# Convolution and state projections of a scan block on tiles of the TensorE array, with other ranks

## The chip, the cores and the metric

The kernel runs on one core of a Trainium2 chip. The metric is device time in microseconds for one call, the median of three runs. A separate execution was recorded by the profiler; its own time and its span are given beside the runs, and all durations of single instructions come from it.

## The reference

The input `x` is 8 images of 96 channels and 64 x 64 positions (L = 4096), in f32. There are two layers. The first is a selective-scan block:

```python
xh = _layernorm(transpose(_gn(x)))
xi, z = split(xh @ in_proj_w.T + in_proj_b, 2)            # 192 channels each
xi = silu(depthwise_conv3x3(xi, conv_w) + conv_b)
xs = [xi by rows, xi by columns, and both reversed]       # k = 0..3
dts, Bs, Cs = split(einsum('bkdl,kcd->bkcl', xs, x_proj_w), [6, 22])
delta = softplus(einsum('bkrl,kdr->bkdl', dts, dt_proj_w) + dt_proj_b)
h = exp(delta * A) * h + delta * xs * Bs                  # 16 states, along L
y = sum(h * Cs) + Ds * xs                                 # the four k summed back in place
out = (layernorm(y) * silu(z)) @ out_proj_w.T + out_proj_b
x = x + out
```

The second layer takes tokens t of 96 channels: an attention without softmax (so keys and values reduce to one 96 x 96 matrix per image), then a feed-forward of 384 hidden units whose operands are rounded to an 8-bit float. Both are added to t.

## The kernel before

The images are worked in four pairs. The channels of a pair, 2 x 192, are held as three tiles of 128 partitions, T = 0, 1, 2: T = 0 has the first 128 channels of one image, T = 1 those of the other, T = 2 the last 64 of each. Positions go in chunks of F = 512 (eight rows of an image), so an image has NCH = 8 chunks.

**Stages.** For each pair there is a front part, then a scan, then a back part. The program alternates: a stage with the front part of pair 0; a scan; three middle stages in which the back part of one pair and the front part of the next are mixed; a scan after each; and a last stage with only a back part. The scan (`scan`) is a loop written out by hand and is not touched.

**The front part** consists of `project`, `convolve` and `prepare`. `project` normalises chunks and multiplies them with the input weights (three matmuls a chunk), writing `xi` into padded images `pad[T]` and the gate `z` to DRAM. `convolve` does the 3 x 3 depthwise convolution. T = 0 and T = 2 are done on VectorE, nine passes over half an image each (L521, L524). T = 1 is done on TensorE (L532): per chunk nine matmuls with diagonal 128 x 128 weights (`diag`, made at L506) into one PSUM bank, evicted by ScalarE with the bias; then one ScalarE SiLU per chunk and T. `prepare` works on 32 sets (k, c), direction k and chunk c. A set does three matmuls (L594) of 128 x 76 weights into one bank: B, C and the 6 rank rows of both images, summed over T. ScalarE copies the 76 rows to `S`. B and C go to DRAM (`bs`, `cs`). Three matmuls with 12 rows (L606) give the step sizes of each T. For each T follow a softplus, a product `du` on VectorE (L611), and a split of the f32 step into three bf16 parts: ScalarE copy, VectorE difference (L622), ScalarE copy, GpSimd difference (L627). They go to DRAM as `du` and `dl`. For the column directions (k = 1, 3), GpSimd first makes the transposed chunk (L586).

**The back part** consists of `back` and `tail`. `back` works on 16 units (chunk and image): it reads the scan's `ys`, adds directions (L923, on VectorE and GpSimd), transposes by matmuls with the identity (`turn`, L937, into `py` banks), normalises, gates and projects out (`both`, L956), normalises again and builds keys and values (`keys`, L989; `outer`, L996; copies to `kv`). When all 16 units are done, `hm` is formed, and `tail` does 16 units of attention and feed-forward (L1046, L1054, L1065), each with a norm (L394, L398).

**Order.** Within a stage no order is written by hand. Each operation is recorded in a `Plan` with its engine, an assumed cost, what it reads and writes, the rings of buffers it takes from, and a rank. `Plan.run` then simulates the engines: for each engine it takes, among the operations that could start within 0.1 us of the earliest, the one with the lowest rank, and emits it. So each engine's queue is an order that was fixed when the program was built, and each engine executes it strictly in turn. All DMAs are issued by SyncE's queue. The ranks of a stage run from 0 to about 1, and constants set where each part lies: the front up to FRONT, convolution to CONV, sets from PREP to 1, back up to BACK, tail from TAIL to TAIL_END. A change of SiLU, softplus or logarithm costs ScalarE a table load.

**PSUM** has eight banks. In a middle stage there are rings `q` (3), `hold` (2) and `py` (2), and `pm` has one. The convolution and L594 use `py` in a middle stage and `hold` in the first.

## Time and profile before

| what | us |
|---|---|
| median of 3 runs (10441.0 to 10453.86) | 10443.78 |
| the profiled execution | 10465.3 |
| its span | 10463.5 |
| first stage, to the first scan instruction | 571 |
| each scan | 1778 |
| each middle stage | 784, 788, 785, and 25 to the next scan |
| last stage | 346 |

Busy over the whole span: PE (matmul) 7723.3 us, VectorE 9031.7, ScalarE 6996.6, GpSimd 8006.9; the DMA queue's packets take 76.2% of the 16 engines' span.

A line of a group gives source line, engine, operation, the tiles written and read by the program's names, the shape, the count, then busy us and mean ns of one, then the idle time of the engine just ahead of it and what ended that. An f32 matmul stands in the profile as two records. Lines of helpers stand for many calls: L287 is every ScalarE activation, L306 every DMA of a stage. `A` is a slab that holds many tiles of the front part. In rows by stretches of time, the columns are from and to, the length, then busy time with the number of instructions for PE, PE weight loads, VectorE (DVE), ScalarE (ACT) and GpSimd (POOL), then the TensorE clock granted as a share of full speed, the mean busy share of the DMA engines, and GB/s.

### The profile page before, as it was taken

The numbers are of one execution on the slowest core, as the hardware profiler recorded it, in microseconds if no ns is written. First come the engines' busy times: TensorE is split into PE (matmuls) and PEld (weight loads), VectorE is DVE, ScalarE is ACT, GpSimd is POOL, SyncE is SP. The second block draws the span as 40 slices with busy tenths as digits, with TensorE's granted clock in tenths as the row PEclk, the third lists the DMA queues.
The fourth block names the chain that finished last, engine by engine and source line by source line (L and its number), as shares of the span: only waits on it lengthen the run. The fifth ranks groups of instructions, "written<-read, shape, count | busy, mean of one in ns | idle before, by whom it ended". The sixth has DMA issues, their size and how long they took to land. (4 is left out here: it accounts for less than half of the span.)

```text
span 10463.5 us, 377190 instructions
## 1 busy us (share of the span) xinstructions
PE 7723.3 (74%) x163328; PEld 5391.4 (52%) x163328; DVE 9031.7 (86%) x6692; ACT 6996.6 (67%) x12229; POOL 8006.9 (77%) x2799
## 2 busy tenths in 40 slices
PE   7856667668986667666997666666699766666678
PEld 2245556554425556555432555555543255555554
DVE  6589999997569999999655999999865699999985
ACT  4567777765666777776666777777656677777754
POOL 3489999990349999998133999999713499999971
PEclk8689898999878998998986889998898699989889
DMA  4888888877868888887686888888767688788884
GB/s 119 213 212 215 213 215 213 217 193 158 217 164 214 212 216 214 215 216 191 164 211 163 212 212 216 215 213 215 191 166 207 167 214 214 215 216 213 215 194 104
DMA packets 1590580, 2082.95 MB, mean 199 GB/s; under 512 B 406579, under 2 KB 1047092, under 8 KB 1585332
## 3 DMA queue, kind: packets, MB, share of 16 engines
q1 hardware_dynamic: 1588916, 2058.80, 76.2%
q8 instruction: 1283, 21.02, 0.9%
q14 instruction: 381, 3.12, 0.1%
HBM read 1600.53 MB, written 457.72 MB: 197 GB/s over the span
## 5 line engine op out<-in xcount | busy, mean ns | idle before, releaser
L794 DVE TENSOR_TENSOR_SCAN h<-da,dbu 128x774 f32<-128x774 f32 x4096 | 7027.0, 1759 | 132.2 <-POOL dbu L758 30.7
L758 POOL TENSOR_TENSOR dbu<-dut,bc 128x1536 f32<-128x1536 f32 x2048 | 7082.5, 3547 | 68.4 <-DMA cw<-cs 23.3
L783 ACT ACTIVATE da<-da 128x768 f32<-128x768 f32 x4092 | 3260.4, 797 | 1995.4 <-PE da L776 1985.5
L776 PE MATMUL da<-dm,aw 128*128 128x128 bf16 x24576 | 2288.5, 236 | 2270.9 <-DVE h L794 2056.7
L776 PEld LDWEIGHTS <-aw 128*128 128x128 bf16 x24576 | 1794.5, 104 | 2516.7 <-issue 2212.3
L812 PE MATMUL yp<-h,cw 128*32 128x48 f32 x131072 | 2910.7, 239 | 86.9 <-issue 73.3
L812 PEld LDWEIGHTS yp<-h,cw 128*32 128x32 f32 x131072 | 2417.0, 154 | 537.4 <-issue 220.7
L712 ACT ACTIVATE cw<-bc,blk 128x512 f32<-128x512 f32 x2048 | 1472.7, 720 | 76.1 <-DMA dm<-dl 57.0
L627 POOL TENSOR_TENSOR A<-A 128x512 bf16<-128x512 f32 x384 | 469.4, 1226 | 960.3 <-ACT A L287 940.3
L287 ACT ACTIVATE A<-A 128x512 bf16<-128x512 f32 (+2 forms) x809 | 486.2, 619 | 235.3 <-DVE A L622 229.9
L923 POOL TENSOR_TENSOR yd<-yk 128x768 f32<-128x768 f32 x64 | 131.1, 2048 | 626.8 <-DMA yk<-ys 357.1
L606 PE MATMUL q<-A 12*128 12x512 f32 x768 | 517.5, 786 | 57.2 <-ACT A L287 50.7
L820 ACT ACTIVATE yev<-yp 128x384 f32<-128x384 f32 x1024 | 504.7, 493 | 65.2 <-PE yp L812 64.8
L622 DVE TENSOR_TENSOR A<-A 128x512 f32<-128x512 f32 x384 | 338.6, 887 | 206.0 <-ACT A L287 193.5
L586 POOL COPY A<-A 128x512 f32<-128x512 f32 x96 | 143.0, 1501 | 364.8 <-ACT A L287 318.7
L755 ACT COPY dbu<-h 128x12 f32<-128x12 f32 x1984 | 409.5, 206 | 0.0
L606 PEld LDWEIGHTS q<-A 12*128 12x128 f32 x768 | 147.3, 223 | 368.0 <-ACT A L287 209.0
L937 PEld LDWEIGHTS py<-ident,yd 128*96 128x96 f32 x2048 | 262.8, 176 | 134.7 <-issue 89.7
L611 DVE TENSOR_TENSOR A<-A 128x512 f32<-128x512 f32 x192 | 188.4, 989 | 149.1 <-ACT A L287 148.6
L1073 POOL TENSOR_TENSOR yk<-yk,yd 96x512 f32<-96x512 f32 x64 | 89.7, 1404 | 294.4 <-DVE yd L1071 240.9
L937 PE MATMUL py<-ident,yd 128*96 128x128 f32 x2048 | 284.9, 291 | 24.7 <-DVE yd L923 11.2
L524 DVE SCALAR_TENSOR_TENSOR A<-A,c_convw,A 128x2048 f32<-128x2048 f32 x128 | 299.6, 2380 | 0.2
(131 smaller groups left out, 5916.1 us busy)
## 6 DMA issues: line engine op xcount, KB each, us to landing
dut<-du SPq DMA_DIRECT2D x2048, 384.0 KB
dm<-dl SPq DMA_DIRECT2D x1024, 288.0 KB
dl<-A SPq DMA_DIRECT2D x256, 384.0 KB
dm<-dl SPq DMA_DIRECT2D x1024, 96.0 KB
ys<-yev SPq DMA_DIRECT2D x1024, 96.0 KB
du<-A SPq DMA_DIRECT2D x256, 256.0 KB
bc<-cs SPq DMA_DIRECT2D x512, 128.0 KB
bc<-bs SPq DMA_DIRECT2D x512, 128.0 KB
```

What stands on the lines that cost most here:

```text
L287: "ACT", cost, lambda: nc.scalar.activation(dst(), src_(), func, **kw),
L606: mm(P, 1.0, lambda pq=pq, k=k, T=T, S=S: nc.tensor.matmul(P[pq], dtw[64:76, k, T], P[S][64:76], start=True, stop=True), (S, "dtw"), (pq,) ...
L627: P.add("POOL", 1.24, lambda rest=rest, dp=dp, w=w: nc.gpsimd.tensor_tensor(P[dp][:, :, 2], w(rest), P[dp][:, :, 1], ALU.subtract), (rest, ...
L712: nc.scalar.activation(cw[i % 2][:, :, :, m, :].rearrange("p z j t -> p (z j) t"), bc[i][:, 1].rearrange("p z (j t) -> p (z j) t", j=NB), ...
L755: nc.scalar.copy(start, segs(hs[s - 1][:, :, r])[:, :, :, 1 if back else TC])
L758: nc.gpsimd.tensor_tensor(segs(t)[:, :, :, 1:], dut[g].unsqueeze(1) .to_broadcast([128, 2, NI, TC]), bc[s // NB][:, 0, :, bass.ts(c % NB, ...
L776: nc.tensor.matmul(e[:, i], aw[k, r][:, i, z, :], dm[s // 2][:, NI * r + i, bass.ts(c % 2, TC)], start=True, stop=True,)
L783: nc.scalar.activation(e, e, AF.Exp)
L794: nc.vector.tensor_tensor_scan(hs[s][:, w, r][:, d], da[p % 3][:, o : o + W6][:, d], dbu[4 * s + r][:, w][:, d], 0.0, ALU.mult, ALU.add,)
L812: nc.tensor.matmul(y[32 * q : 32 * q + 32, 2 * NE * i : 2 * NE * i + 2 * NE] .rearrange("p (j r i) -> p i j r", j=2, r=NR), w[:, z, :, t], ...
L820: nc.scalar.activation(yev[s][:, :, o : o + 8, :].rearrange("p j i e -> p i j e"), y[:, 0 : 16 * NE].rearrange("p (i j e) -> p i j e", j=2 ...
L937: nc.tensor.matmul(o, P[yd][:, k, j, DIM * g : DIM * g + DIM], ident, start=(k + j == 0), stop=(k + j == 4),)
```

## The change

The convolution of T = 1 no longer uses 128 x 128 diagonal weights but 32 x 32 ones (`diag` is 128 x 9 x 32). Four chunks of an image half are done in one block (`taps`): for each of nine taps, 16 matmuls, one for each group i of 32 channels and each chunk j. Channel group i is rows 32i of the array and writes bank i; chunk j is columns 32j and partitions 32j of the bank. The block needs four banks at once. ScalarE evicts each 32-partition piece with SiLU and bias directly (bias from `cbr`, laid out for it), so the separate SiLU of T = 1 falls away.

In `prepare`, the first product (`states`) puts one image into columns 0 to 63 and the other into columns 64 to 127: two matmuls for T = 0 and T = 1 side by side, then two for T = 2. The bank has 128 rows, in which each image's 6 rank rows come first and then B and C; these go to DRAM in two DMAs each instead of one. The weights `xw` grow from 76 to 128 columns; they are prepared once in `weights`. The second product (`steps_`) is six matmuls of 6 rows and 64 columns at rows 0, 64, 32 and 96 of the array, into three banks. `dtw` is loaded in four pieces to these rows. A ring `set` lets two sets be between `states` and `steps_` at a time.

`Plan` gets `claims`: a claimed operation that is ready but short of banks keeps operations of higher rank from taking banks of that ring. The banks are now `q` (5) and `hold` (2), with 3 `hold` in the first stage; `py` is gone. The ranks FRONT, CONV, PREP, BACK, TAIL and TAIL_END have other values.

```diff
@@ -36,12 +36,12 @@
 SEG = TC + 1
 W6 = NI * SEG
 HQ = TC // 4
-FRONT = 0.22
-CONV = 0.28
-PREP = 0.24
-BACK = 0.65
-TAIL = 0.54
-TAIL_END = 0.65
+FRONT = 0.13
+CONV = 0.27
+PREP = 0.15
+BACK = 0.63
+TAIL = 0.85
+TAIL_END = 1.33
 NE = 24
 X0 = F - 3 * SEG
...
         self.unit = self.also = None
+        self.claims = set()
...
@@ -108,7 +109,12 @@
                 heirs[j].append(i)
         ready = [i for i, n in enumerate(owed) if not n]
         while ready:
-            best = {}
+            best, claimed = {}, {}
+            for i in self.claims & set(ready):
+                rings = [self.home[n] for n in self.ops[i][4] if n not in self.tiles]
+                for ring in set(rings):
+                    if len(self.free[ring]) < rings.count(ring):
+                        claimed[ring] = min(claimed.get(ring, 9.0), self.ops[i][5])
             for i in ready:
                 engine, cost, _, after, uses, rank, kind, _ = self.ops[i]
...
@@ -116,7 +122,7 @@
                 for ring in {self.home[n] for n in uses if n not in self.tiles}:
                     want = sum(self.home[n] == ring for n in uses if n not in self.tiles)
                     slots = sorted(f[0] for f in self.free[ring])
-                    short |= len(slots) < want
+                    short |= len(slots) < want or (i not in self.claims and rank > claimed.get(ring, 9.0))
                     at = max([at] + slots[:want])
                 if short:
...
     convw = load("convw", [128, 2, 9], -0.8)
     convb = load("convb", [128, 2], 0.1)
+    cbr = const.tile([128, 4], F32, name="cbr")
+    for j in range(4):
+        lay(cbr[32 * j : 32 * j + 32], a["convb"][:, 0:1].rearrange("(i p) o -> p (i o)", i=4), 0.1, "cb")
...
         for out_, in_, rank, name, after in later:
             dma(P, 0.1, lambda out_=out_: out_, lambda in_=in_: in_, after, (f"w_{name}",), (), rank)
-        xw = wp.tile([128, KD, 3, 76], F32, name="xwp")
+        xw = wp.tile([128, KD, 3, 128], F32, name="xwp")
+        P.add("POOL", 1.4, lambda: nc.gpsimd.memset(xw, 0.0), (), ("xwp",), (), -0.5)
+        parts = []
...
+        dma(P, 0.79, lambda: xwd, lambda: xw, parts, ("xwd",), (), 0.1)
...
-        diag = p1.tile([128, 9, 128], F32, name="diag")
-        for t in range(9):
-            dve(P, 0.28, lambda t=t: nc.vector.tensor_scalar(
-                diag[:, t, :], ident, convw[:, 0, t : t + 1], None, ALU.mult), ("w_convw",), (f"diag#{t}",), (), -0.5)
+        diag = p1.tile([128, 9, 32], F32, name="diag")
+        for g in range(4):
+            g4 = slice(32 * g, 32 * g + 32)
+            dve(P, 0.45, lambda g4=g4: nc.vector.tensor_tensor(
+                diag[g4], ident[g4, g4].unsqueeze(1).to_broadcast([32, 9, 32]),
+                convw[g4, 0].unsqueeze(2).to_broadcast([32, 9, 32]), ALU.mult),
+                ("w_convw",), (f"diag.{g}",), (), -0.5)
         for h in range(2):
             first = FRONT + (CONV - FRONT) * h / 2
...
                             o, v, w, o, ALU.mult, ALU.add), (), wr, (), first + (CONV - FRONT) / 2 * (9 * (T // 2) + t) / 18)
-            for c in range(4 * h, 4 * h + 4):
-                first = FRONT + (CONV - FRONT) * c / 8
-                r0 = c * ROWS
-                n = f"pc.{c}"
+            first = FRONT + (CONV - FRONT) * h / 2
+            ns = [f"pc{h}{i}" for i in range(4)]
+
+            def taps(h, ns):
                 for t in range(9):
                     dy, dx = divmod(t, 3)
-                    mm(P, 0.87, lambda n=n, t=t, r0=r0, dy=dy, dx=dx: nc.tensor.matmul(
-                        P[n], diag[:, t, :], pad[1][:, r0 + dy : r0 + dy + ROWS, dx : dx + HH],
-                        start=(t == 0), stop=(t == 8)), (f"diag#{t}", "edge1", *[f"pad1#{j}" for j in range(NCH)]), (n,), ((n, "py" if beside else "hold"),), first)
-                act(P, lambda c=c: xi[1][:, bass.ts(c, F)], lambda n=n: P[n], AF.Identity, 0.68, (n, "A1.1", "w_convb"),
-                    (f"xi1#{c}",), (), first, bias=convb[:, 0:1])
+                    for j in range(4):
+                        r0 = (4 * h + j) * ROWS + dy
+                        for i in range(4):
+                            g4 = slice(32 * i, 32 * i + 32)
+                            nc.tensor.matmul(
+                                P[ns[i]][32 * j : 32 * j + 32], diag[g4, t],
+                                pad[1][g4, r0 : r0 + ROWS, dx : dx + HH], start=(t == 0), stop=(t == 8),
+                            )
+
+            P.claims.add(len(P.ops))
+            mm(P, 9.0, lambda h=h, ns=ns, taps=taps: taps(h, ns),
+               ("edge1", *[f"pad1#{c}" for c in range(NCH) if h or c <= NCH // 2],
+                *[f"diag.{g}" for g in range(4)]), ns, [(n, "q") for n in ns], first)
+            for i in range(4):
+                for j in range(4):
+                    g4 = slice(32 * i, 32 * i + 32)
+                    j4 = slice(32 * j, 32 * j + 32)
+                    act(P, lambda g4=g4, c=4 * h + j: xi[1][g4, bass.ts(c, F)], lambda n=ns[i], j4=j4: P[n][j4],
+                        AF.Silu, 0.6, (ns[i], "A1.1", "w_cb"), (f"xi1#{4 * h + j}.{i}",), (), first,
+                        "silu", bias=cbr[j4, i : i + 1])
         P.also = None
         for c in range(NCH):
-            for T in range(3):
-                b_ = 0.0 if T == 1 else convb[:, half(T) : half(T) + 1]
+            for T in (0, 2):
+                b_ = convb[:, half(T) : half(T) + 1]
                 act(P, lambda T=T, c=c: xi[T][:, bass.ts(c, F)], lambda T=T, c=c: xi[T][:, bass.ts(c, F)],
                     AF.Silu, 0.72, ("w_convb",), (f"xi{T}#{c}",), (), FRONT + (CONV - FRONT) * (0.5 if c < 4 else 1), "silu", bias=b_)
+
...
         P.also = "A2" if beside else "A3"
-        xw = tmp.tile([128, KD, 3, 76], F32, name="xw")
-        dma(P, 0.5, lambda: xw, lambda: xwd, ("xwd",), ("xw",), (), -1)
-        dtw = tmp.tile([128, KD, 3, 128], F32, name="dtw")
-        dma(P, 0.1, lambda: dtw[64:76], lambda: a["dtw"].rearrange("k r t c -> r k t c"), (), ("dtw",),
-            (), -1)
+        xw = tmp.tile([128, KD, 3, 128], F32, name="xw")
+        dma(P, 0.79, lambda: xw, lambda: xwd, ("xwd",), ("xw",), (), -1)
+        dtw = tmp.tile([128, KD, 128], F32, name="dtw")
+        places = ((0, 0, 0, 0, 128), (64, RK, 1, 0, 128), (32, 0, 2, 0, 64), (96, RK, 2, 64, 64))
+        for at, r, T, o, n in places:
+            dma(P, 0.03, lambda at=at, o=o, n=n: dtw[at : at + RK, :, o : o + n],
+                lambda r=r, T=T, o=o, n=n: a["dtw"][:, r : r + RK, T, o : o + n].rearrange("k r c -> r k c"),
+                (), (f"dtw{at}",), (), -1)
         ring(P, tmp, "S", 2, [128, F])
+        P.ring("set", [None] * 2)
         for T in range(3):
...
                     pt, S = "pt" + n, "S" + n
-                    for T in range(3):
-                        mm(P, 1.0, lambda pt=pt, k=k, T=T, f=u[T]: nc.tensor.matmul(
-                            P[pt][:76], xw[:, k, T], f(), start=(T == 0), stop=(T == 2)),
-                           (un[T], "xw"), (pt,), ((pt, "py" if beside else "hold"),), rank)
-                    act(P, lambda S=S: P[S][:76], lambda pt=pt: P[pt][:76], AF.Copy, 0.59, (pt,), (S,),
+
+                    def states(pt, k, u):
+                        for last in (False, True):
+                            for b in range(2):
+                                h = slice(64 * b, 64 * b + 64)
+                                nc.tensor.matmul(
+                                    P[pt][h], xw[:, k, 2 if last else b, h], u[2 if last else b](),
+                                    start=not last, stop=last,
+                                )
+
+                    P.unit = f"set.{k}.{c}"
+                    mm(P, 1.9, lambda pt=pt, k=k, u=u, states=states: states(pt, k, u),
+                       (*un[0], *un[1], *un[2], "xw"), (pt,), ((pt, "q"),), rank)
+                    act(P, lambda S=S: P[S], lambda pt=pt: P[pt], AF.Copy, 0.59, (pt,), (S,),
                         ((S, "S"),), rank)
-                    for v, r in ((bs, 0), (cs_, 32)):
-                        dma(P, 0.07, lambda v=v, k=k, c=c: v[k, 2 * c : 2 * c + 2].rearrange("j p t -> p j t"),
-                            lambda S=S, r=r: P[S][r : r + 32].rearrange("p (j t) -> p j t", j=2),
-                            (S,), (), (), rank)
+                    for v, r in ((bs, RK), (cs_, 32 + RK)):
+                        for b in range(2):
+                            dma(P, 0.035, lambda v=v, k=k, c=c, b=b: v[
+                                    k, 2 * c : 2 * c + 2, NS * b : NS * b + NS].rearrange("j p t -> p j t"),
+                                lambda S=S, r=r, b=b: P[S][64 * b + r : 64 * b + r + NS].rearrange(
+                                    "p (j t) -> p j t", j=2), (S,), (), (), rank)
+                    pqs = [f"pq{n}.{T}" for T in range(3)]
+
+                    def steps_(pqs, k, S):
+                        for at, T, o in ((0, 0, 0), (0, 0, 64), (64, 1, 0), (64, 1, 64), (32, 2, 0), (96, 2, 64)):
+                            nc.tensor.matmul(
+                                P[pqs[T]][o : o + 64], dtw[at : at + RK, k, o : o + 64], P[S][at : at + RK],
+                                start=True, stop=True,
+                            )
+
+                    mm(P, 1.2, lambda pqs=pqs, k=k, S=S, steps_=steps_: steps_(pqs, k, S),
+                       (S, *[f"dtw{at}" for at, *_ in places]), pqs, [(q, "q") for q in pqs], rank)
+                    P.unit = None
                     for T in range(3):
                         m = f"{n}.{T}"
                         pq, d, q, dp, rest = "pq" + m, "d" + m, "du" + m, "dp" + m, "rest" + m
-                        mm(P, 1.0, lambda pq=pq, k=k, T=T, S=S: nc.tensor.matmul(
-                            P[pq], dtw[64:76, k, T], P[S][64:76], start=True, stop=True),
-                           (S, "dtw"), (pq,), ((pq, "q"),), rank)
                         act(P, lambda d=d: P[d], lambda pq=pq: P[pq], AF.Softplus, 0.675, (pq, "w_dtb"), (d,),
                             ((d, "d"),), rank, "softplus", bias=dtb[:, k, half(T) : half(T) + 1])
...
                 for g in range(2):
                     py = f"py{g}" + n
                     mm(P, 1.0, lambda yd=yd, k=k, g=g, py=py, turn=turn: turn(yd, k, g, py), (f"{yd}#{k}",),
-                       (py,), ((py, "py"),), rank)
+                       (py,), ((py, "q"),), rank)
             for g in range(2):
...
             P = Plan()
             tmp = st.enter_context(tc.tile_pool(name="bk", bufs=1))
             if new and old:
-                psum = banks(P, st, q=3, hold=2, py=2)
+                psum = banks(P, st, q=5, hold=2)
             elif new:
-                psum = banks(P, st, q=4, hold=4)
+                psum = banks(P, st, q=5, hold=3)
             else:
-                psum = banks(P, st, q=3, hold=2, py=2)
+                psum = banks(P, st, q=5, hold=2)
```

## Prediction

> **What bounds the kernel now.** I read the page first, then the busy time by stage, then one middle stage cut at its own events, then its groups of instructions and its waits.
>
> The page, parts 1 and 2:
>
> ```profile
> PE 7723.3 (74%) x163328; PEld 5391.4 (52%) x163328; DVE 9031.7 (86%) x6692; ACT 6996.6 (67%) x12229; POOL 8006.9 (77%) x2799
> ...
> PE   7856667668986667666997666666699766666678
> ...
> DVE  6589999997569999999655999999865699999985
> ...
> PEclk8689898999878998998986889998898699989889
> ```
>
> The shares of the whole mislead: DVE's 86% are the four scans. In the dips of the DVE row (slices 10-12, 20-22, 30-32) PE shows 7 to 9. By stage: 0 to 571 us the first front stage, four scans of 1778 us, three middle stages (2349 to 3133, 4936 to 5724, 7530 to 8315, each with 25 us to the next scan), the last stage 346 us. The scans are built from the same instructions after the change, so I take nothing from them, and the last stage's order on PE is the same with other PSUM tiles; both count as 0. What can move is 3 x 785 us and 571 us.
>
> One middle stage, cut at the first matmul, the first and last convolution matmul, the end of the back part, and the scan; columns are time, length, then busy us (instructions) of PE, weight loads, DVE, ACT, POOL, then clock, DMA share, GB/s:
>
> ```profile
> 2372.00:2551.00 179.00, 167.27 (x627) 87.69 (x628) 131.22 (x162) 123.80 (x191) 19.31 (x10) 0.96 0.84 186
> 2551.00:2629.00 78.00, 77.97 (x223) 36.94 (x222) 46.31 (x30) 33.08 (x48) 5.82 (x6) 1.00 0.37 91
> 2629.00:2937.00 308.00, 286.34 (x779) 119.78 (x780) 171.25 (x221) 196.45 (x319) 103.21 (x80) 0.84 0.82 215
> 2937.00:3133.00 196.00, 168.57 (x294) 50.64 (x293) 121.87 (x210) 134.91 (x223) 71.98 (x56) 0.71 0.58 156
> ```
>
> PE is 86 to 100% busy in all four phases, 705 of 784 us, and no other engine is above 74% in any. PE sets this stage. But DMA is second: 0.82 at 215 GB/s in the third phase, and 0.71 over the stage, which is 557 us of work at full share. That is the next floor. The groups that the change touches, in the same stage:
>
> ```profile
> L606 PE MATMUL q<-A 12*128 12x512 f32 x192 | 125.8, 767 | 9.5 <-ACT A L287 7.4 <-DVE yk L1048 1.6 <-ACT small L287 0.3
> ...
> L532 PE MATMUL py<-A,diag 128*128 128x512 f32 x144 | 63.4, 592 | 0.0
> L594 PE MATMUL py<-A 128*76 128x512 f32 x96 | 60.8, 741 | 0.9 <-POOL A L586 0.9
> ...
> L594 PE MATMUL py<-A,A 128*76 128x512 f32 x96 | 55.7, 703 | 2.6 <-DVE yt L949 1.9 <-ACT A L287 0.7
> ```
>
> Each f32 matmul is two records, so L532 is 72 matmuls of 0.88 us (clock 1.00), and the projections are 96 + 96 for 242.3 us: 7.57 us for each of the 32 sets (k, c) of `prepare`. Together 306 of PE's 705 us.
>
> **Convolution on 16 tiles.** 72 matmuls become 288 on 32x32 tiles, 18 rows of 16. If 16 run together a row costs one stream of 512 columns, 0.88 us: 15.9 us, -47.5 us. Nothing before shows row tiles at work. Column tiles are shown by the scan's L812 (48 columns, four column tiles in turn):
>
> ```profile
> 1002.50 1.51 PE L812 MATMUL yp<-h,cw 128*32 128x48 f32 x64
> ...
> 1010.97 0.69 PE L812 MATMUL yp<-h,cw 128*32 128x48 f32 x32
> ```
>
> 48 columns alone would stream 48/512 x 0.44 = 41 ns per record at full clock. Taking off some 0.2 us for the last one's way through, 32 records stand 15 ns apart, and 64 at the half clock (82 ns alone) 20 ns apart: four tiles do overlap, and a record can be issued every 15 to 18 ns. A row of 16 tiles is 32 records, at most 0.58 us of issue, under the 0.88 us of streaming. So issue doesn't bind. The bounds: no overlap at all, 288 x 0.88 = 253 us (+190); columns only, 63 us (0); full, 15.9. The Trainium skill, "TensorE: Matmul & The Clock Gate", section Measured speedup vs the span model, gives 10.6x for 16 tiles of 512 columns: 288 x 0.88 / 10.6 = 24 us, an estimate, -39. L812 is near to full overlap, so I take 16 to 18 us.
>
> **Projections on tiles.** A set was 3 + 3 streams; now two pairs on 64-column tiles (two streams) and six matmuls on six tiles (one). At the stage's clock of 0.84 a stream is 0.88/0.84 = 1.05 us; with the fill of the first, 3.3 us for 7.57: -137 us in 32 sets. Without any overlap it is ten streams, 10.5 us (+94). One rule speaks against it: "TensorEngine Tiling (Array Packing)", Gotcha 1: PSUM Pressure, says that different row tiles can't be in the same PSUM bank at once, and the two halves of T=2 (rows 32 and 96) write one bank. No row here shows that. If it holds, a set has a fourth stream: 34 us less gain, -103. I keep -137, since PE is no longer the floor in either case.
>
> PE after: 705 - 47 - 137 = 521 us, in a stage of 784.
>
> **The other edits.** ACT: 8 evictions (0.687) and 8 SiLUs (0.623) of T=1 go, 32 SiLUs of 32 partitions come. A 64-partition eviction takes 0.68, so partitions give nothing back; 32 x 0.62 = 19.8 against 10.5, +9.3 us. The order on ACT has 47 table loads for 56: -9 x 1.283 = -11.5. ACT stays at 487. DVE: nine 0.476 us products become four smaller ones, about -2. SP gets 64 more issues of 0.4 us (26 us of a queue that issues some 600 in 784 us), behind which dl and du wait; it is covered as long as SP waits for its producers, which are its longest waits. The bytes don't change; `dtw` in four loads and the wider `xw` come once a stage, before their readers, and the memset, the 16 extra DVE copies and `cbr` once, in the first stage, under its waits for `x` and `awd`.
>
> **The claim on PSUM.** A convolution half takes four of the five `q` banks at once, is let past later work to get them, and holds them over 9 us of matmuls and 16 SiLUs (10 us). All other `q` work, `turn`, `both`, `keys` and half of each norm, has one bank meanwhile, and PE's queue stands behind the block. That can idle PE for 0 to 15 us a half. I take 0: in those 40 us DVE's taps end last, and the back units that come later run into a phase that DMA sets. Without this cover it costs up to 30 us a stage.
>
> **Ranks.** Here lies most of the doubt. In the order of before, 73% of the sets' matmuls stand ahead of the back part's end, after the change 34%: ACT has 69 of 96 softplus after the last `kv` copy, where it had 32. So the last phase gets heavier while the earlier ones shrink. By phase, for the new order:
> - To the first set. The front is ahead of the back now (5.3 of 16 back units before the convolution, for 7.1), which takes about 1.8 x 14.4 = 26 us of PE off, and the convolution's PE time no longer stands between. DVE's 36 taps last 85 us; they ended 49 us after the last front matmul, and would again: at about 2575 instead of 2629.
> - To the end of back. 9.5 back units and 9 sets. PE: 9.5 x 14.4 + 9 x 3.1 = 165 us. DMA: a unit reads and writes 2.95 MB, a set 2.1 MB, `us` 6.3 MB, less 5 MB loaded ahead: 48 MB. 215 GB/s at 0.82 is 260 at full share, so 48 MB at 0.85 is 217 us. DMA sets it; end at 2792.
> - The last phase. 23 sets and 16 tail units. DMA: 23 x 2.1 + 16 x 0.59 = 57.7 MB, 261 us at 0.85. ACT: 140 copies x 0.624, 69 x 0.679, 20 x 0.586, 16 loads x 1.283, and the tail's 30.3 + 28.5 + 9.3 = 235 us, 276 at 85%. PE: even at the half clock (1.76 us per f32 stream, 0.44 for the tail's fp8), 23 sets of 3 streams and 16 units of 3 + 6: 248 us. I take 276. End at 3068.
>
> So the middle stage goes from 784 to about 722: -62. A check by bytes alone: 104 MB are left at 2575, and at 217 GB/s they end at 3054.
>
> PE's clock speaks against more: the first stage already shows what comes when PE isn't the floor.
>
> ```profile
> 300.00:400.00 100.00, 83.66 (x112) 20.87 (x110) 55.99 (x65) 60.01 (x106) 39.19 (x34) 0.63 0.88 225
> 360.00:380.00 20.00, 13.38 (x14) 2.98 (x12) 12.06 (x14) 11.51 (x22) 7.22 (x7) 0.51 0.92 237
> 440.00:540.00 100.00, 73.16 (x98) 17.88 (x96) 55.36 (x62) 55.79 (x97) 46.32 (x39) 0.64 0.81 209
> ```
>
> At 360 us PE is 67% busy at half clock and DMA runs at 237 GB/s: sets leave at 8.6 to 9.5 us each whatever PE does. **The first stage** therefore gains only its head: the convolution's 49 us of PE among the first sets, where POOL's last piece of a set first ran at 222 us. Sets could flow from about 190; 73 MB at 218 GB/s then end at 525 to 533, for 550: -20 us (bounds 0 and -45).
>
> **Sum** against the profiled 10465.3 us (span 10463.5): 3 x 62 + 20 = 206, so 10259. The median of the runs is 21.5 below the profiled one: 10238, said as 10240.
>
> **Rivals.**
> - *DMA packs tighter.* The stretch 2750 to 2800 had 0.94 at 242 GB/s. 104 MB at 242 end at 3005; ACT at 92% in the last phase (255) ends at about 3020: -113 a stage, -40 in the first: about 10065. For: more independent work. Against: the first stage, which averaged 0.835 with nothing else to do.
> - *Columns overlap, rows don't.* The convolution gains nothing, a set is 2 + 4 streams at worst: the change doesn't do what it says. Only the ranks and the lighter pairs help, -30 a stage: 10350.
> - *The late sets end the stage (the other side).* In the last phase, two sets at a time go through PE, ACT, DVE, ACT, POOL and SP beside a tail whose table differs. If a set with its share of tail takes over (3133 - 2792)/23 = 14.8 us, where ACT needs 10.2 and DMA 11.3, the stage is longer than before; at 16 us it is +27, together 3 x 27 - 20 = +61: 10505. For: ACT reached 69% and DMA 0.58 in this phase before. Against: PE was 86% busy then, at clock 0.71. Short of that point, at 14 us, it is -19 x 3 - 20: 10367.
> - *No tile overlaps.* +190 + 94 on the engine that bounds: about +250 a stage: 11400. L812 speaks against it.
>
> **Chances.** My forecast 0.53 (own range 10180 to 10300), tighter DMA 0.20, columns only 0.05, late sets short of the point 0.13, beyond it 0.06, no overlap 0.03. Within 0.2%, about what a measurement of this kernel tells from no change, falls a small part of the late sets: 0.03. So faster 0.88, same 0.03, slower 0.09. The range leaves out the two slower cases and half of the tight one: 10080 to 10400.
>
> **What would show it.** Convolution matmuls in two blocks of 8 to 10 us; 3 to 4 us of PE per set; PE under 75% of a middle stage; DMA at 0.8 or above from the first set on; the back part ending near 2790 and ACT the busiest engine after it. I am wrong if the tiles' records follow one another, if the last phase passes 340 us, or if it ends well under 260.

## The result and the profile after

The changed kernel takes 10315.64 us, the median of four runs (10309.3 to 10321.7), beside 10447.66 for the kernel before (10441.0 to 10453.86): a ratio of 0.9874, with a 95% interval of 0.9857 to 0.9891. That is 132 us less. I had said 10240 and a range of 10080 to 10400. The direction holds and the time lies in the range, but it lies outside the likeliest case's own range (10180 to 10300): about two thirds of the gain came.

The page of the kernel after, parts 1 and 2, with the rows that I showed of before:

```profile
PE 7289.4 (71%) x166080; PEld 5185.1 (50%) x166080; DVE 9045.2 (88%) x6688; ACT 7000.9 (68%) x12268; POOL 8011.6 (78%) x2800
...
PE   6766666768866666676886666767688567666678
...
DVE  6589999997579999999767999999866799999985
...
PEclk7579999898868999989986989898898798999999
```

PE lost 434 us of busy time. In slices 10 to 12, 20 to 22 and 30 to 32, the dips of the DVE row, it now shows 8, 8 and then 6, 6 or 5, with a clock digit of 6, 6 or 7 in the last of each three. The profiled execution is 10309.3 us with a span of 10307.5, 156 us under the span of before (whose profiled execution was itself 18 us above its median, so the stages sum to more than the 132 of the medians). The times at which the scans begin and end tell where these 156 us lie: the first stage is 571.2 us before and 549.4 after (-22). The three middle stages, each with its passage into the next scan, are 810.0, 813.7, 810.0 before and 774.2, 758.8, 769.8 after (-36, -55, -40). The four scans (-2) and the last stage (-2) are as they were.

One middle stage, the first one, cut at the start of the stage, the first set, the end of the back part (`hm`) and the end; columns as before. First the kernel after, then the kernel before at the same events:

```profile
2328.40:2581.50 253.10, 206.34 (x1452) 108.56 (x1452) 176.85 (x192) 161.59 (x245) 28.38 (x30) 0.89 0.66 155
2581.50:2794.90 213.40, 183.58 (x791) 88.00 (x792) 111.12 (x158) 117.27 (x192) 47.29 (x35) 0.88 0.80 207
2794.90:3077.60 282.70, 205.81 (x616) 53.55 (x612) 206.37 (x289) 206.21 (x352) 143.44 (x103) 0.70 0.76 205
```

```profile
2348.60:2628.90 280.30, 250.59 (x1097) 129.69 (x1097) 185.83 (x209) 157.86 (x240) 28.22 (x30) 0.94 0.68 155
2628.90:2937.40 308.50, 286.84 (x779) 119.92 (x780) 171.72 (x223) 196.85 (x319) 103.31 (x80) 0.84 0.82 215
2937.40:3133.60 196.20, 168.17 (x294) 50.60 (x292) 121.89 (x209) 135.01 (x224) 72.13 (x57) 0.71 0.58 156
```

The head is 27 us shorter, the middle phase 95 shorter, the last phase 87 longer: 36 in all. PE, busy 93% in the middle phase before, is at 86% there and at 73% in the last phase, where DVE and ACT are at 73% too and DMA at 0.76. No engine is above 86% in these two phases any more. The three middle stages of this one execution differ by up to 15 us (774, 759, 770) although every engine runs the same instructions in the same order in all three, so a difference between two kernels in a single stage is worth less than one that all three stages or the medians show. The touched groups, in the same stage (line, engine, operation, tiles, shape, count, busy us, mean ns, idle time ahead and its releasers):

```profile
L657 PE MATMUL q<-A 6*64 6x512 f32 x384 | 72.7, 763 | 16.2 <-ACT A L296 15.3 <-ACT yd L296 0.7
L637 PE MATMUL q<-A 128*64 128x512 f32 x128 | 49.4, 915 | 16.3 <-ACT A L296 15.1 <-ACT small L296 0.6 <-ACT yd L296 0.4
L637 PE MATMUL q<-A,A 128*64 128x512 f32 x128 | 42.9, 810 | 1.5 <-DVE yt L1008 1.3 <-ACT A L296 0.2
L552 PE MATMUL q<-A,diag 32*32 32x512 f32 x576 | 21.1, 596 | 1.3 <-ACT small L296 1.3
```

The convolution (L552) fell from 63.4 to 21.1 us of PE, the projections (L637 and L657) from 242.3 to 165.0. That is 120 us; PE as a whole went from 705.6 to 595.7 in this stage, 110 less.

### The profile page after: what moved, and what is told of

The parts are those of the page before. It is cut to its first block, busy times and chain, and to the rows that moved or that the text cites. A ratio compares the mean times of both kernels' runs of the same rounds, so it can differ in the third digit from the quotient of the medians.

```text
span 10307.5 us, 383249 instructions
## 1 busy us (share of the span) xinstructions
PE 7289.4 (71%) x166080; PEld 5185.1 (50%) x166080; DVE 9045.2 (88%) x6688; ACT 7000.9 (68%) x12268; POOL 8011.6 (78%) x2800
## 5 line engine op out<-in xcount | busy, mean ns | idle before, releaser
L296 ACT ACTIVATE A<-A 128x512 bf16<-128x512 f32 (+1 forms) x777 | 466.4, 620 | 274.0 <-DVE A L681 228.4
L657 PE MATMUL q<-A 6*64 6x512 f32 x1536 | 331.6, 779 | 74.3 <-ACT A L296 70.4
L996 PEld LDWEIGHTS q<-ident,yd 128*96 128x96 f32 x2048 | 238.6, 165 | 84.1 <-issue 53.1
L996 PE MATMUL q<-ident,yd 128*96 128x128 f32 x2048 | 255.1, 276 | 17.3 <-DVE yd L982 9.5
L637 PE MATMUL q<-A 128*64 128x512 f32 x512 | 209.5, 935 | 77.3 <-ACT A L296 56.6
L296 ACT ACTIVATE small<-hold 96x512 f32<-96x512 f32 x192 | 112.7, 590 | 218.5 <-PE hold L407 218.3
```

Source lines behind the costliest of these rows:

```text
L296: "ACT", cost, lambda: nc.scalar.activation(dst(), src_(), func, **kw),
L657: nc.tensor.matmul(P[pqs[T]][o : o + 64], dtw[at : at + RK, k, o : o + 64], P[S][at : at + RK], start=True, stop=True,)
L996: nc.tensor.matmul(o, P[yd][:, k, j, DIM * g : DIM * g + DIM], ident, start=(k + j == 0), stop=(k + j == 4),)
```

## The experiments

All differences below are of medians of runs on the same chip beside the kernel before, which is given each time. "Stage" is a middle stage with its passage into the scan; its mean of three is 811 before and 768 after.

**The parts apart.** Four kernels. The kernel before with only the six new constants:

```diff
-FRONT, CONV, PREP, BACK, TAIL, TAIL_END = 0.22, 0.28, 0.24, 0.65, 0.54, 0.65
+FRONT, CONV, PREP, BACK, TAIL, TAIL_END = 0.13, 0.27, 0.15, 0.63, 0.85, 1.33
```

> The kernel before with nothing changed but the six rank constants. Theory A (the tiles took PE off the path, the ranks do little or harm while PE is the floor): 10430 to 10520 us. Theory B (the order made the gain, the tiles little): 10320 to 10390 us. PE's work stays at about 705 us in a middle stage.

The kernel after with the six old constants (the same diff the other way round):

> The changed kernel with the six old rank constants: tiles and banks alone. Theory A: within 40 us of the changed kernel, 10290 to 10360 us, since more sets stand ahead of the back part's end and the last phase gets shorter by what the earlier ones get longer. Theory B: most of the gain is lost, 10400 to 10450 us.

The kernel after with the projections as before (`xw` of 76 columns, three + three matmuls and two DMAs of B and C a set), so tiles in the convolution alone, with the new banks, claim and ranks:

```diff
-for last in (False, True): for b in range(2): matmul(P[pt][h], xw[:, k, 2 if last else b, h], ...)
+for T in range(3): matmul(P[pt][:76], xw[:, k, T], u[T], start=T == 0, stop=T == 2)
```

> The changed kernel with the projections as before (three matmuls of 76 columns, three of 12 rows a set), so the convolution on 16 tiles, the banks and the ranks alone. Theory A: PE loses 42 of the 119 us of matmul work that the tiles save in a middle stage, so about a third of the gain, 10390 to 10430 us. Theory B: 10310 to 10350 us.

And the kernel after with the convolution as before, so without the claim too, but with the new banks:

```diff
-taps(h, ns): 16 matmuls of 32x32 a tap, four chunks in one block, claimed
+for c in range(4 * h, 4 * h + 4): nine matmuls of diag[:, t, :] (128 x 128) into one bank of q
```

> The changed kernel with the convolution as before (72 matmuls of 128x128, an eviction and a SiLU of its own, no claim), so the projections on tiles, the banks and the ranks alone. Theory A: PE loses 77 of 119 us in a middle stage, two thirds of the gain, 10350 to 10390 us; in the first stage the convolution's 40 us of PE come back and with them most of the 22 us won there. If the claim on four banks costs what the gap between the two blocks suggests (16 us a middle stage), this is as fast as the changed kernel, 10310 us.

| kernel | median us | ratio to before (10446.32) | first stage | middle stages | first set, end of back, end (middle stage 1, us from its start) |
|---|---|---|---|---|---|
| ranks alone | 10516.89 | 1.0068 (1.0053 to 1.0083) | 579 | 823, 828, 825 | 276, 612, 823 |
| all tiles, old ranks | 10447.74 | 1.0002 (0.9991 to 1.0013) | 559 | 810, 806, 809 | 302, 500, 810 |
| convolution on tiles, new ranks | 10428.1 | 0.9982 (0.9975 to 0.9989) | 584 | 791, 791, 794 | 252, 610, 791 |
| projections on tiles, new ranks | 10303.41 | 0.9864 (0.9848 to 0.9880) | 547 | 763, 766, 766 | 276, 456, 763 |

So the new order alone costs 70 us, the tiles alone give nothing, and both together give 132. Theory A fits the first and the third of these kernels and theory B the second, so neither explains the gain by itself. "Tiles alone" has the new banks, the ring `set` and the claim in it as well; the banks and that ring were not run apart. The projections with the ranks give all of it; the convolution on tiles adds nothing to them (10303 against 10316; the intervals of the two ratios overlap). Why, the phases show. All tiles with the old ranks, then tiles in the convolution alone, each from the first set on:

```profile
2637.70:2835.20 197.50, 170.36 (x733) 77.09 (x736) 117.91 (x161) 123.26 (x202) 52.81 (x41) 0.88 0.79 205
2835.20:3120.70 285.50, 204.26 (x576) 51.14 (x570) 186.47 (x274) 189.41 (x325) 124.13 (x98) 0.72 0.69 185
```

```profile
2612.80:2971.00 358.20, 325.83 (x888) 146.98 (x888) 200.35 (x251) 222.29 (x361) 128.98 (x95) 0.79 0.83 214
2971.00:3127.00 156.00, 126.51 (x268) 40.37 (x267) 104.47 (x190) 108.23 (x190) 54.21 (x45) 0.83 0.61 167
```

With the old ranks the two phases after the first set take 483 us, even less than the 496 of the kernel after, but the first set starts at 302 instead of 253: with those ranks back work goes ahead of the front, the last front matmul starts at 222 (after: 183), DVE's taps end at 275 (after: 242). The new ranks are worth this head. With the old projections PE is 91% busy for 358 us: there it is still the bound, and the new ranks' mix of sets and back work is long.

Projections on tiles alone, all three phases:

```profile
2323.10:2598.90 275.80, 241.89 (x1052) 124.67 (x1052) 181.43 (x201) 158.37 (x238) 34.76 (x30) 0.94 0.64 147
2598.90:2779.20 180.30, 160.55 (x760) 79.94 (x760) 111.85 (x154) 119.11 (x191) 49.81 (x35) 0.95 0.88 239
2779.20:3060.80 281.60, 203.55 (x616) 51.92 (x612) 207.91 (x290) 205.66 (x353) 144.28 (x103) 0.71 0.77 205
```

This answers what the convolution's tiles bring: the first set comes 23 us later without them, but the phase behind it is 33 us shorter, with DMA at 0.88 and 239 GB/s instead of 0.80 and 207 for about the same bytes (43 and 44 MB). In the second and third stages that phase is 21 and 26 us shorter. The end is 11 us earlier in this stage, on the mean of three 2.4 us. The 42 us that the tiles take off PE are real and are given back in the phase that follows. That this phase is slower with them is measured; which instruction in it waits more isn't shown.

**The claim.**

```diff
-            P.claims.add(len(P.ops))
```

> The changed kernel without the claim, so that a convolution block gets its four banks only when four are free by chance. If the claim idles PE for nothing, the stage gets up to 16 us shorter: 10260 to 10310 us. If the claim is what lets the block run at all beside the back part, the block comes later and with it all sets: 10350 us and above.

10362.98 us, 0.9917 (0.9902 to 0.9932) of 10455.7: 47 us slower than with the claim. The two convolution blocks stood where they stood (193 to 230 us from the stage's start), and so did the first set (251). What changed is the planner's order after them: the last phase has 3 table loads on ACT where it had 15, and lasts 307 us instead of 283, with DMA at 0.70:

```profile
2781.60:3088.70 307.10, 212.54 (x600) 53.38 (x596) 196.45 (x283) 193.45 (x334) 129.67 (x103) 0.71 0.70 188
```

In the first stage, where the order is the same on every engine, the two kernels take 551 and 549 us. So the time lies in the range that was given for a late block, but the block isn't late: what the claim is worth here is the order that the planner happens to find with it. The 47 us measure that order, and not what the claim costs PE, so that cost, which had been named as a reason why the projections alone might be as fast, isn't shown. The 47 us do show what an order alone can do, which the next experiments need.

**What binds the late phases?** Three kernels, one that puts a load on and two that take one off. The first writes every `du` twice (the second write to the same place):

```diff
-spread(P, 0.26, ... duv[k, j, ...])
+for _ in range(2): spread(P, 0.26, ... duv[k, j, ...])
```

> The changed kernel with every write of du issued twice to the same place: 25 MB and 128 SP issues more in each stage with a front part, nothing else. If DMA sets the stretch from the first set to the end (0.76 to 0.79 busy there), each such stage grows by about 25 MB at 235 GB/s, 100 us: 10650 to 10720 us. If DMA has slack there and the chains of the sets set it, the 30 MB that its idle share could carry take most of it: under 40 us a stage, 10310 to 10450 us.

11253.63 us, 1.0766 (1.0748 to 1.0784). It lies outside both ranges and doesn't decide what it was made for. A second write to the same place waits for the first to land, in SP's queue. The queue's waits of this kernel from 0 to 600 us (total us, times, longest):

```profile
SPq L315 <- DMA du<-A: 156.1, 66, 4.7
```

Each such wait takes 2.4 us of a queue in which everything else stands behind. From 260 to 600 us the DMA engines were at 0.67, under the 0.87 of the kernel after, so bytes weren't tried at all. What it shows is the price of a landing on this queue.

The second leaves out the second ScalarE copy and the third part of the split (its place is filled with zeros), 60 us of ACT in a stage; the third leaves out the matmuls of T = 2 in `states`:

```diff
-act(..., P[dp][:, :, 1], rest, AF.Copy)          # then POOL: rest - second part
+dve(..., P[dp][:, :, 1] = d - first part)        # POOL: d - d
```

> The changed kernel without ScalarE's second copy of each step size: VectorE's difference is written as the second bf16 part at once, and the third part is left out (GpSimd writes zeros in the same time). ScalarE loses 96 copies of 0.625 us a stage, and each chain of a set one link; bytes, PE, VectorE and GpSimd stay. If ScalarE or the chain through it sets the stretch, 30 to 60 us a stage go: 10080 to 10200 us. If DMA sets it: 10280 to 10320 us.

```diff
-for last in (False, True): for b in range(2): ...
+for b in range(2): matmul(P[pt][h], xw[:, k, b, h], u[b], start=True, stop=True)
```

> The changed kernel without the two T=2 matmuls of states (T=2's part of B, C and the ranks is left out), so a set has two streams on PE instead of three, some 40 us of PE less in a stage. If PE still sets the stage: 20 to 40 us a stage, 10160 to 10250 us. If not: 10290 to 10320 us.

Less ACT work: 10262.98 (0.9820, 0.9806 to 0.9835), stages 756, 753, 757, so 12 us a stage on the mean of three for 49 us less on ACT (436 for 485). Less PE work: 10282.98 (0.9841, 0.9826 to 0.9855), 756, 756, 758, so 11 us a stage for 22 us less on PE (573 for 596); in its last phase the granted clock fell to 0.63, from 0.70, and PE stayed busy 198 of 277 us:

```profile
2776.30:3053.10 276.80, 197.79 (x536) 48.14 (x532) 207.65 (x289) 206.19 (x351) 142.58 (x103) 0.63 0.78 209
```

Both times lie between the ranges that the two theories were given. Without the PE work, ACT, DVE and POOL run the order of the kernel after, so this difference is that of the work. Without the ACT work the order moved too (13 table loads in the last phase for 15), and a link of every chain went with the load, so its 12 us aren't divided between load, link and order. Neither engine alone is the bound. The likely reading is that each is a link of a chain; that is argued from the waits of the kernel after, last phase of the stage (who waited for whom, us in total, times, longest):

```profile
POOL A L686 <- ACT A L296: 113.1, 39, 7.2
ACT A L296 <- DVE A L681: 31.1, 31, 3.3
...
PEld q L657 <- ACT A L296: 29.8, 26, 2.9
```

POOL waits for ACT, ACT for DVE, PE for ACT: the split's steps, one after another, each engine at 50 to 73%. Which of these waits sets the end of the stage isn't shown.

**The queue and the bytes.** One DMA of all 112 rows of `S` per set instead of four of 16 rows: 96 issues fewer in a stage, 3.1 MB more:

```diff
-for v, r in ((bs, RK), (cs_, 32 + RK)): for b in range(2): dma(v[...], P[S][64 * b + r : 64 * b + r + NS])
+dma(bs[k, 2 * c : 2 * c + 2], P[S][RK : RK + 112])
```

> The changed kernel with one DMA for B and C of both images in a set instead of four: rows 6 to 117 of S go as they stand to one scratch tensor, which the scan reads in pieces of the same size as before. 96 SP issues of some 0.57 us (55 us of SP's queue) less in each stage with a front part, 3.1 MB (12 us of DMA at full share) more. Theory Q (SP's one queue, which issues 73% of the last phase and waits for producers in the rest, sets it): 15 to 40 us a stage, 10160 to 10260 us. Theory D (bytes): 10310 to 10360 us. Theory L (latency of the chains at full rings): 10290 to 10320 us.

The same on top of the kernel with tiles in the projections alone:

> The version with the projections on tiles and the convolution as before, with the one DMA a set: if theory Q holds, it beats both kernels and all so far, 10130 to 10240 us; if not, 10290 to 10320 us.

And 128 small issues more (four rows of `S` a set to a place that nobody reads), almost no bytes:

```diff
+for q_ in range(4): dma(P, 0.001, spare_[k, c, q_ : q_ + 1], P[S][q_ : q_ + 1], (S,), (), (), rank)
```

> The changed kernel with four more DMAs in each set, each of one partition of 2 KB from S to a tensor that nobody reads: 128 SP issues a stage (about 64 us of SP's queue), 0.26 MB. Theory Q: 30 to 64 us a stage longer, 10430 to 10570 us. Theories D and L: 10310 to 10350 us.

| kernel | median us | ratio to before (10454.87) | stages | first stage |
|---|---|---|---|---|
| one DMA | 10405.96 | 0.9953 (0.9938 to 0.9968) | 796, 793, 800 | 557 |
| one DMA, projections alone | 10402.57 | 0.9949 (0.9930 to 0.9967) | 795, 798, 790 | 553 |
| 128 issues more | 10367.81 | 0.9917 (0.9895 to 0.9939) | 778, 778, 778 | 575 |

Fewer issues didn't help: 90 and 99 us worse than the kernels that they were made from, and outside every theory's range. More issues cost 10 us a middle stage and 25 in the first, though few bytes come with them. In a middle stage the order moved a little with them. In the first stage the order is almost that of the kernel after, so its 25 us can be put down to the issues. From 260 us to near the end of the first stage, first the kernel after, then with 128 issues more:

```profile
260.00:510.00 250.00, 191.25 (x516) 38.93 (x516) 147.90 (x162) 154.71 (x269) 118.52 (x100) 0.59 0.87 226
```

```profile
260.00:535.00 275.00, 187.66 (x532) 38.63 (x528) 141.62 (x166) 161.68 (x273) 119.46 (x101) 0.61 0.81 212
```

The DMA share falls from 0.87 to 0.81. In these two stretches SP's queue spends 194 of 250 us on issuing DMAs in the kernel after and 240 of 275 us with 128 issues more (78% and 87%; in the last phase of a middle stage it is 175 of 283 us in the kernel after); with one DMA a set it is 127 of 253 us from 265 us on (50%). So the queue slows this stage when it gets more to issue, but it wasn't the limit before: at 50% the sets flow no faster. From the first to the last run of POOL's last piece of a set the first stage takes 298 us with one DMA a set and 298 in the kernel after; the 8 us more of the first stage (557 for 549) lie ahead of that.

That the one DMA is slower in the middle stages is partly settled by the order. With tiles in both, the planner found nearly the order of the kernel without the claim: an instruction's place in its engine's queue differs by 0.4% of the queue on average from that kernel, by 2.0% from the kernel after, and the last phase has 4 table loads for 15. That order alone took 783 us a stage for 768; with the one DMA it is 796. So about half of the difference goes with the order, and some 14 us a stage stay open. With the projections alone the order moved less (0.4%; 69 of 96 softplus in the last phase for 68), and yet the middle phase took 204 us for 180 and the last 290 for 282. `S` has two buffers, and a larger DMA may hold one longer; or the 3.1 MB (14 us at 215 GB/s) do it in part. A third buffer wasn't tried.

## Why the prediction was right, and where its sizes were off

**Which stages move: right.** Scans and last stage counted 0 and gave -2 each. The first stage was put at -20 and gave -22. The middle stages were put at -62 each and gave -36, -55 and -40, mean -44: the whole shortfall lies there. Of the signs that I had named, the two blocks came. The others did not: PE is busy 80% of the first middle stage and not under 75%, a set costs PE 5.2 us and not 3 to 4, DMA is at 0.76 in the last phase, and the back part ends 466 us into the stage and not near 441.

**The first stage: right by luck.** I had let the sets flow from about 190 us at a rate that PE doesn't touch. The mark that I used was POOL's last piece of a set. Before, and after:

```profile
L627 POOL TENSOR_TENSOR A<-A x96: 1145/1154/1601, 223.3 to 546.1; 128x512 bf16<-128x512 f32 x96
```

```profile
L686 POOL TENSOR_TENSOR A<-A x96: 1142/1154/1602, 225.7 to 524.2; 128x512 bf16<-128x512 f32 x96
```

The first piece is no earlier; DVE's taps still end at 215 us, for 218. The gain is in the flow, 298 us for 323 or 9.3 us a set for 10.1, and DMA moves 226 GB/s in the row of the kernel after above, where before it moved 214:

```profile
262.00:540.00 278.00, 229.57 (x328) 59.49 (x326) 155.45 (x173) 160.66 (x282) 121.80 (x102) 0.67 0.84 214
```

So "whatever PE does" was wrong. The parts say which work it was: the flow takes 298 and 301 us in the two other kernels with the projections on tiles, 311 and 330 us in the two without.

**The head of a middle stage was mis-sized.** I put the first set at 226 us; it came at 253. This is about as much as stage 1 fell short. I had the last front matmul 26 us earlier than before: it was 19 (183.4 for 202.5). I had the taps' end 49 us after it: it was 59. And I let the sets begin at the taps' end: 11 us more went by. They can be read line by line in the timeline of the kernel after (start, length, engine, operation, tiles; in brackets what its engine waited for):

```profile
2568.52 2.34 DVE L540 SCALAR_TENSOR_TENSOR A<-A,c_convw,A 128x2048 f32<-128x2048 f32 x1
...
2574.20 1.28 ACT L296 ACT_TABLE_LOAD   x1
...
2575.49 1.34 ACT L296 ACTIVATE A<-A,c_convb 128x512 f32<-128x512 f32 x2
...
2577.47 1.33 ACT L296 ACTIVATE A<-A,c_convb 128x512 f32<-128x512 f32 x2
...
2578.00 3.62 PE L1015 MATMUL q<-g,c_woT 96*96 96x512 f32 x4
...
2581.55 1.98 PE L637 MATMUL q<-A,A 128*64 128x512 f32 x4
```

The last tap ends at 2570.86. ACT first finishes a norm of the back part and changes its table, so the SiLU of the chunk starts at 2575.49; then PE has an output product of the back part ahead in its queue, and the first `states` starts at 2581.55. In-order queues put work of the back part between, which my step had left out.

**The two later phases were right in size, not in reason.** The back part's end came 213 us after the first set (said: 217) and the last phase took 283 (said: 276), 12.3 us for each of 23 sets (said: 12.0). But DMA, which I had set the first by, carried 44 MB at a share of 0.80 where I had put 48 MB at 0.85: two errors that cancel. The kernel with tiles in the projections alone moved about the same bytes in 180 us, and came from its first set to the end in 462 us, where my check by bytes alone gives 479. In the last phase I took 276 from 235 us of ACT at 85%. ACT is busy 206 of 283 us (the durations add to 231, but they overlap), DVE is level with it, and PE has 206 us, not 248. No load that I had named fills this phase, so that its size came out is luck in part; what sets it stays open.

**Convolution on tiles: the mechanism right, the size off, the worth wrong.** It comes in two blocks, as said. The first of the two rows here holds the first block (four records at 2521.2, a wait, then 284 records from 2523.5 to 2533.8); in the second PE waits between the blocks, with a clock of 0.67:

```profile
2521.00:2534.00 13.00, 11.73 (x291) 6.38 (x291) 13.00 (x10) 4.05 (x6) 3.65 (x1) 1.00 0.15 48
2534.00:2549.70 15.70, 11.41 (x26) 4.58 (x25) 11.99 (x8) 13.60 (x20) 0.00 (x0) 0.67 0.17 50
```

The blocks lasted 10.3 and 9.8 us, so a row of 16 tiles takes 1.1 us rather than one stream of 0.88. I said 15.9 and took 16 to 18; it is 20.1 in blocks and 21.1 in busy time, in the middle between full overlap and the 24 us estimated from the Trainium skill's 10.6x ("TensorE: Matmul & The Clock Gate", Measured speedup vs the span model): 253 / 21.1 is 12.0x. Rows and columns of tiles both overlap, so the rival in which only columns do has fallen. But the step that made these 42 us into an earlier end failed: the kernel without them is no slower.

**Projections on tiles: the clock was mis-sized.** I took 3.3 us a set at a clock of 0.84; it is 165.0 / 32 = 5.2 us. Three streams at the half clock of 1.76 us each would be 5.3. Most sets now run late, in the phase with a clock of 0.70, at some 5.4 us each; but in the middle phase, with a mean clock of 0.88, it is already 4.7. In both phases many sets run at the half clock: the two streams of one `states` take 1.9 us in 12 of the 32 sets and 3.5 to 3.7 in 14. The mean clock of a phase was not the clock of its sets. That the tiles themselves overlap is plain at full clock. The six matmuls of one `steps_`, twelve records:

```profile
2586.14 1.10 PE L657 MATMUL q<-A 6*64 6x512 f32 x12
```

One stream is 0.88. The two halves of T = 2, rows 32 and 96 of the array, write one bank (different partitions of it), and no fourth stream is to be seen here: the Trainium skill's rule that I had weighed against it ("TensorEngine Tiling (Array Packing)", Gotcha 1: PSUM Pressure) doesn't hold for this case. PE of the stage is 596 us instead of 521. As forecast it is no longer the floor by itself: 22 us less PE work in the kernel without T = 2 moved 11 us.

**Ranks and the claim.** I had called the ranks the largest doubt and put their worth in an earlier head and a heavier last phase. Both came: the head 27 us shorter, the last phase 87 longer. That the ranks alone would lose 70 us I hadn't said. The claim I had costed at 0 to +30 us a stage; without it the kernel is 15 us a stage slower. That is the other order again, so what the claim itself costs PE isn't shown.

**SP's 64 extra issues a stage** I had called covered. Another 128 on top cost 10 us a middle stage and 25 in the first, so there is little room left; but 96 fewer gained nothing in the first stage. What the 64 cost isn't shown.

**The rivals.** DMA packing tighter appeared in the middle phase of variants (0.88 at 239 GB/s with the projections alone), not in the whole. The late sets stayed under the 14 us at which I put the smaller gain.

## What to carry to other kernels

When one engine binds a stage that is ordered once for all engines, relieving it and re-ordering the work are one change: here either alone gave nothing or lost, and both together gave 1.3%. After the relief, don't cost the stage from the next engine's busy time alone: 49 us less on one engine moved 12 us, 22 us less on another moved 11. Look what stands in each queue between the last producer and the first consumer at the seam between two parts: 11 of the 27 us that this forecast lost in the head lie there. And where a planner makes the order, an experiment that changes one operation can change the order too, and that alone was worth 47 us here: compare the orders before a difference is put down to the edit.

## What was not expected of the hardware

- Six matmuls on six tiles, two of them in different rows but in one PSUM bank, took 1.10 us together where one alone streams 0.88.
- Sixteen 32 x 32 tiles run together at 1.1 us a row of 16, 25% over one stream: 288 matmuls in 20.1 us.
- Relief of PE came with a lower granted clock; why isn't shown. In the first stage it was busy 83% at 0.67 before and 77% at 0.59 after; in the last phase of a middle stage 73% at 0.70, and with T = 2 left out 71% at 0.63, for the same 277 to 283 us.
- A write that waits for an earlier one to the same place to land stopped SP's queue for 2.4 us on average, 66 times in the first 600 us.
- A DMA issue took SP's queue about 0.6 us (317 in 194 us). At 87% issuing the first stage was 25 us longer than at 78%; at 50% the flow of its sets was no faster.
